# Transposes of the experts' gathered tokens in fp32r in place of fp32

## The chip, the cores and the metric

The kernel runs on one core of a Trainium2 chip. The metric is the device time of one execution in microseconds (us). The core has five engines that work side by side and meet only at semaphores: TensorE (PE, whose weight loads the profile lists apart as PEld), VectorE (DVE), ScalarE (ACT), GpSimd (POOL) and SyncE (SP), which here issues the plain DMAs.

## The reference

One layer is computed on x of shape (4, 2048, 512), that is 8192 tokens of 512 numbers, all in fp32. To x are added an attention-like map of random features and a mixture of experts; both work on the normalised tokens.

```python
xn = _layernorm(x, axis=-1)
x = x + _L0_attn_ref(xn, ...) + _L0_ffn_ref(xn, ...)

# attention: feats(xn) @ feats(input_weights)^T with 512 features
feats = AB / sqrt(512) * exp(einsum('...d,rd->...r', xw, ab[:, None] * gs) - correction)

# experts: 64 of them, 8 a token, chosen among 4 of 8 groups; room for 256 tokens each
g = jnp.einsum('ech,ehi->eci', dispatch, gate_w)
u = jnp.einsum('ech,ehi->eci', dispatch, up_w)
expert_out = jnp.einsum('eci,eih->ech', jax.nn.silu(g) * u, down_w)
output = jnp.zeros((t, h)).at[tidx].add(gathered * weights)
output = output + (silu(tokens @ shared_gate_w) * (tokens @ shared_up_w)) @ shared_down_w
```

`dispatch` holds, for each expert, the rows of the up to 256 tokens that chose it. An expert has 512 inputs and 256 inner units.

## The kernel before

**Precision.** The products are computed in the type fp32r (`FPR`). To keep the accuracy, the kernel splits each operand into an upper part (`upper`, L96, a cast on ACT to fp32r) and a rest (`rest`, L99, a subtraction on DVE). `products` (L102) then adds three products for each pair of operands: upper by upper, upper by rest, rest by upper. That is why the names come in pairs (`gu_h` and `gu_l`, `gT` twice, `d_h` and `d_l`).

**Transposes.** A product sums over the partitions, so tokens that lie one to a partition have to be turned. `nc.tensor.transpose` does it on TensorE: a tile of 128 x 128 is loaded as the weights, and the identity `ident` (L178, fp32) is passed through. The result lands in PSUM. The tiles of the dense blocks are turned in `turn` (L291, product line L299, PSUM tile `ps_x`), the logits at L344 and the experts' tokens in `turn_slots` (L710, product line L717, PSUM tile `ps_t`). All of these are in fp32 before the change.

**Stages.** The tokens pass in 16 blocks of 512 (`NB`). The first stage, up to some 440 us, normalises and turns them (`normalize`, `look_up`), chooses the experts (`look_up`'s later steps), writes the normalised rows with their scores to `xnw` in DRAM, and computes for every other block the shared expert and the attention (`dense`). The second stage is the loop over the 64 experts at L872. The third, from some 1170 us, computes what was left of the odd blocks (`ends`, L836).

**The loop over the experts.** Step i issues the loads of the gate and up weights of expert i + 2 and the down weights of expert i + 1 on SP's queue (L690, L695). It then computes the inner units of expert i (`hidden`, L735: 48 products of 256 columns into `ps_gu`). Next POOL's queue gets the gather of the tokens of expert i + 4 (`gather`, L698, L702), TensorE turns the tokens of expert i + 1 (`turn_slots`), and ACT and DVE split the weights of expert i + 1 (`split_gates`, L589). Late attention work is drawn from a generator (`late_attention`, L533), in 48 pieces of 12 products spread over the 64 steps by L887, so that 16 steps have none. Last come the output product of expert i - 1 (`down`, L753: 12 products of 512 columns into `ps_e`), its scatter with addition to the output on POOL's queue (L767), and the split of the down weights.

**The step around the change.** `turn_slots(e)` takes the gathered rows `xg` (two tiles of 128 tokens, 577 numbers wide) and makes 8 transposes of 128 x 128. Four of them fill one PSUM tile `ps_t` of 512 columns, of which the pool `ps_tr` has two buffers. After each four, ACT casts the tile to the upper part of `gT` (L97) and DVE subtracts for the rest (L100). So an expert has 8 transposes, 2 casts and 2 subtractions, and the stage has 512, 128 and 128.

**What sets the order.** Each engine runs its own queue in order. The order in a queue is planned when the program is built, from the order of the calls and the dependences, and `behind` (L116) adds edges by hand: at L721 the transposes of expert 0 are put behind what TensorE was given before. `in_turn` (L120) keeps POOL's gathers and scatters in sequence. In the profile the planned order shows: most of the time the 8 transposes stand together behind the 48 products of a step, and at times they are spread among other products.

**Constants.** At the start POOL makes `ident`, `tri`, `tri_r` (a cast to fp32r, L183), `ones_r` (L186) and others, one after the other.

Of the kernel before, what the change touches and what calls it, by code (L numbers as in the profile page):

```python
# [9 lines left out]
FP = mybir.dt.float32  # L10
FPR = mybir.dt.float32r
# [7 lines left out]
P = 128  # L19
# [9 lines left out]
CAP = 256  # L29
# [23 lines left out]
def rfs_attention_moe_kernel(  # L53
# [15 lines left out]
    nc = tc.nc  # L69
    xf = x.flatten_outer_dims()  # L70

    const = ctx.enter_context(tc.tile_pool(name="const", bufs=1))
    dram = ctx.enter_context(tc.tile_pool(name="dram", bufs=1, space=DRAM))
    ps_tr = ctx.enter_context(tc.tile_pool(name="ps_tr", bufs=2, space=PSUM))
# [8 lines left out]
    def kib4(shape, name, dt=FPR):  # L83
        return four.tile(shape, dt, tag="four", name=name)
# [11 lines left out]
    def upper(dst, src):  # L96
        return nc.scalar.copy(dst, src)  # L97

    def rest(dst, src, hi, on=nc.vector):  # L99
        return on.tensor_tensor(dst, src, hi.bitcast(FP), ALU.subtract)  # L100
# [15 lines left out]
    def behind(a, b):  # L116

        tc.add_manual_dep(a.ins, b.ins.name, ORDER, reason="what a needs comes late")
# [58 lines left out]

    ident = const.tile([P, P], FP, name="ident")  # L178
    make_identity(nc, ident)
    tri = kib4([P, P], "tri", FP)  # L180
    make_upper_triangular(nc, tri, 1.0, diag=True)
    tri_r = const.tile([P, P], FPR, name="tri_r")
# [426 lines left out]
    for rc in range(RC):  # L609
        ps = ps_mm.tile([P, H], FP, tag="mm", name="ps_f")  # L610
# [98 lines left out]

    def turn_slots(e):  # L710
        xg = xgs.pop(e)
        gp = [kib4([P, KC, CAP], "gT") for _ in range(2)]
        for c2 in range(KC // 2):
            ps = ps_tr.tile([P, 2, CAP], FP, tag="tr", name="ps_t")
            for c in range(2):
                for h in range(NH):
                    turned_s = nc.tensor.transpose(  # L717
                        ps[:, c, ts(h, P)], xg[:, h, ts(c2 * 2 + c, P)], ident
                    )
                    if e == 0:  # L720
                        behind(turned_s, last["pe"])  # L721
            cs = slice(2 * c2, 2 * c2 + 2)
            upper(gp[0][:, cs, :], ps)
            turned_r = rest(gp[1][:, cs, :], ps, gp[0][:, cs, :])

        we = rt.tile([P, NH], FP, tag="we", name="we", bufs=4)
        shares = nc.vector.scalar_tensor_tensor(
            we, xg[:, :, H + e], 1.0, xg[:, :, H + E], ALU.add, ALU.mult
        )
        behind(shares, turned_r)  # L730
        nc.vector.reciprocal(we, we)
        wes[e] = we
        return gp
# [92 lines left out]
    for n in range(NS):  # L826
# [3 lines left out]
        if n == 0:  # L830
            gws[0] = split_gates(gates.pop(0))
    rest_steps -= RC + NS
    gps[0] = turn_slots(0)
    yes = [kib4([P, NH, H], "ye", FP) for _ in range(3)]

# [36 lines left out]
    for i in range(E + 1):  # L872


        if i + 2 < E:
            gates[i + 2] = load_gates(i + 2)
        if i + 1 < E:
            downs[i + 1] = load_down(i + 1)
        if i < E:
            hps[i] = hidden(i, gps.pop(i), gws.pop(i))  # L880
        next(slots, None)
        if i + 4 < E:
            gather(i + 4)
        if i + 1 < E:
            gps[i + 1] = turn_slots(i + 1)
            gws[i + 1] = split_gates(gates.pop(i + 1))
        for _ in range(rest_steps * i // E, rest_steps * (i + 1) // E):  # L887
            next(rest_of, None)
        if i >= E - 2:
            next(last_of)  # L890
        if i == E:

            next(last_of)
        if i > 0:
            down(i - 1, hps.pop(i - 1), dws.pop(i - 1))
        if i < E:
            dws[i] = split_down(downs.pop(i))
# [40 lines left out]
```

## Time and profile before

| what | value |
|---|---|
| median of three executions | 1355.71 us (1353.23 to 1357.19) |
| the profiled execution | 1351.38 us |
| its span, first to last instruction | 1349.6 us |
| mean granted TensorE clock | 0.993 |
| TensorE busy, first stage (0 to 443 us) | 427.36 us |
| TensorE busy, stage of the experts (443 to 1170 us) | 723.46 us |
| TensorE busy, last stage (1170 to 1350 us) | 171.70 us |
| DMA share in these three stages | 0.57, 0.96, 0.73 |

How to read the profile: a group of instructions is one line, with the source line, the engine, the operation, what it writes and reads (out<-in), its form, how often it ran, its busy time in us and the mean of one in ns; behind the second bar stands how long the engine was idle just before, and what ended that. The forms show fp32 and fp32r operands of TensorE alike as f32; a cast shows its fp32r output. The records of TensorE overlap[...]; the time that one costs is therefore the distance between neighbours and not the length of its record. The chain of work that ended last follows the span back from its end, at each step to what released it. A timeline gives the start in us, the time, the engine and the instruction.

### The profile page before, as it was taken

Reading aid. Unit: us, or ns where it says so; the run is one execution under the profiler, and the core shown is the slowest. Engines: PE = TensorE matmul, PEld = TensorE weight load, DVE = VectorE, ACT = ScalarE, POOL = GpSimd, SP = SyncE. Lnnn points to the kernel's source line nnn. Section 1 sums busy time; section 2 is a strip of 40 time slices with the busy share of each in tenths; the row PEclk is TensorE's granted clock in tenths of the full one; section 3 lists DMA queues with packets and bytes.
Section 4 is the critical chain, followed back from the end, with each engine's and each line's share of the span. In section 5 each row is a group of like instructions: output and inputs, shape, how many; then the busy total and the mean of one; then the engine's idle time right before and its main releaser. Section 6 shows DMA issues by size and latency. Waiting matters only on the chain.

```text
span 1349.6 us, 21219 instructions
## 1 busy us (share of the span) xinstructions
PE 1322.5 (98%) x7648; PEld 1153.4 (85%) x7648; DVE 919.5 (68%) x1898; ACT 647.1 (48%) x1025; POOL 580.0 (43%) x683
## 2 busy tenths in 40 slices
PE   7899999999999899999999999999999999999998
PEld 5788888888888799999999999999999999978886
DVE  5887768768765577767677777767776776544455
ACT  5554433443432365556555655655665566531111
POOL 3322022022004566777667676767677655220000
PEclk9899999999999999999999999999999999999999
DMA  7464544564476899999999999999999989756995
GB/s 248 173 231 166 211 184 157 210 222 161 169 268 200 261 243 286 277 270 272 289 268 257 299 287 263 247 283 286 266 263 289 280 235 273 200 143 231 306 316 203
DMA packets 186265, 327.06 MB, mean 242 GB/s; under 512 B 15536, under 2 KB 87216, under 8 KB 186160
## 3 DMA queue, kind: packets, MB, share of 16 engines
q1 hardware_dynamic: 153392, 245.93, 53.0%
q0 software_dynamic: 32768, 79.78, 26.6%
q8 instruction: 60, 0.98, 0.3%
q14 instruction: 45, 0.37, 0.1%
HBM read 220.66 MB, written 104.99 MB: 241 GB/s over the span
## 4 chain that ended last, share of the span: by engine, by line
PE 91%; DMA 3%; DVE 2%; POOL 2%; ACT 1%; issue 1%; SPq 0%; DVEq 0%; POOLq 0%; ACTq 0%
PE ps_gu L107 40%; PE ps_e L107 13%; PE ps_o L107 13%; PE ps_f L107 6%; PE ps_y L107 5%; PE ps_fu L107 5%; PE ps_t L717 4%; PE ps_l L327 2%; PE ps_x L299 2%; DMA at<-upto,line 1%; DMA rw_sb<-in_L_ffn_router_w_dram 1%; POOL at L649 1%; DMA xT_l<-turned 1%; PE ps_lt L344 0%; DVE r L460 0%
## 5 line engine op out<-in xcount | busy, mean ns | idle before, releaser
L107 PE MATMUL ps_gu<-gT,gu_h 128*128 128x256 f32 x2048 | 295.1, 284 | 0.0
L767 POOL DMA_INDIRECT out_dram<-ye,who x128 | 217.4, 1698 | 142.0 <-DMA out_dram<-ye,who 41.1
L107 PEld LDWEIGHTS ps_gu<-gT,gu_h 128*128 128x128 f32 x2048 | 269.3, 192 | 7.0 <-ACT gu_h L97 2.5
L702 POOL DMA_INDIRECT xg<-xnw,who x128 | 143.4, 1121 | 96.1 <-issue 72.1
L649 POOL DMA_INDIRECT at<-upto,line x128 | 148.0, 1156 | 82.5 <-DVE xb L506 43.8
L107 PE MATMUL ps_gu<-gT,gu_l 128*128 128x256 f32 x1024 | 167.1, 285 | 0.0
L100 DVE TENSOR_TENSOR gu_l<-gu,gu_h 128x1024 fp32r<-128x1024 f32 x128 | 155.4, 1216 | 3.8 <-ACT gu_h L97 3.8
L107 PE MATMUL ps_e<-d_h,ehT 128*128 128x512 f32 x512 | 148.8, 392 | 0.0
L107 PEld LDWEIGHTS ps_gu<-gT,gu_l 128*128 128x128 f32 x1024 | 140.9, 192 | 2.8 <-DVE gu_l L100 2.7
L97 ACT CAST gu_h<-gu 128x1024 fp32r<-128x1024 f32 x128 | 131.5, 1056 | 0.0
L97 ACT CAST ehT<-sg 128x512 fp32r<-128x512 f32 x64 | 39.8, 622 | 179.2 <-DVE sg L460 179.2
L228 POOL TENSOR_TENSOR a<-rstd,ve 128x4 f32<-128x4 f32 x48 | 10.9, 227 | 265.4 <-DVE rstd L226 262.8
L107 PEld LDWEIGHTS ps_e<-d_h,ehT 128*128 128x128 f32 x512 | 94.9, 188 | 19.0
L766 ACT ACTIVATE ye<-ps_e,we 128x512 f32<-128x512 f32 x128 | 87.9, 693 | 33.9 <-PE ps_e L107 33.9
L460 DVE SCALAR_TENSOR_TENSOR sg<-sg,ps_gu 128x512 f32<-128x512 f32 x64 | 44.0, 688 | 81.5 <-PE ps_gu L107 81.2
L100 DVE TENSOR_TENSOR d_l<-d,d_h 128x1024 fp32r<-128x1024 f32 x64 | 78.2, 1222 | 11.3 <-ACT d_h L97 11.2
L458 ACT ACTIVATE sg<-ps_gu 128x512 f32<-128x512 f32 x64 | 38.2, 597 | 96.2 <-PE ps_gu L107 95.6
L100 DVE TENSOR_TENSOR gT<-ps_t,gT 128x512 fp32r<-128x512 f32 x128 | 83.3, 682 | 0.4 <-ACT gT L97 0.4
L107 PE MATMUL ps_e<-d_l,ehT 128*128 128x512 f32 x256 | 79.1, 390 | 1.0 <-DVE d_l L100 1.0
L107 PE MATMUL ps_o<-fW_h,fT 128*128 128x512 f32 x288 | 79.7, 391 | 0.3 <-ACT fT L97 0.2
L107 PE MATMUL ps_o<-d_h,hT 128*128 128x512 f32 x256 | 79.8, 399 | 0.0
L717 PE MATMUL ps_t<-ident,xg 128*128 128x128 f32 x512 | 76.1, 275 | 3.5 <-DVE gT L100 3.5
(172 smaller groups left out, 2534.2 us busy)
## 6 DMA issues: line engine op xcount, KB each, us to landing
gu<-in_L_ffn_gate_w_dram SPq DMA_DIRECT2D x64, 512.0 KB
gu<-in_L_ffn_up_w_dram SPq DMA_DIRECT2D x64, 512.0 KB
d<-in_L_ffn_down_w_dram SPq DMA_DIRECT2D x64, 512.0 KB
xnw<-xw SPq DMA_DIRECT2D x32, 577.0 KB
xb<-in_L_attn_x_dram SPq DMA_DIRECT2D x32, 512.0 KB
out_dram<-xb SPq DMA_DIRECT2D x32, 512.0 KB
xT_h<-turned SPq DMA_DIRECT2D x30, 512.0 KB
xT_l<-turned SPq DMA_DIRECT2D x30, 512.0 KB
```

The source lines that it names most:

```text
L97: return nc.scalar.copy(dst, src)
L100: return on.tensor_tensor(dst, src, hi.bitcast(FP), ALU.subtract)
L107: last["pe"] = nc.tensor.matmul(ps, w[c][a], v[c][b], start=(start and part == 0 and c == 0), stop=(stop and part == 2 and c == n - 1),)
L299: last["turn"] = nc.tensor.transpose(ps[:, ts(s, P)], src(s)[:, ts(kc, P)], ident)
L327: logits = nc.tensor.matmul(pl, rwp[:, kc].rearrange("p t e -> p (t e)"), v[kc], start=(n == 0 and kc == 0), stop=(n == 1 and kc == KC - 1),)
L458: nc.scalar.activation(dst, g, AF.Tanh, scale=0.5)
L460: nc.vector.scalar_tensor_tensor(dst, dst, 0.5, u, ALU.mult, ALU.mult)
L649: nc.gpsimd.indirect_dma_start(out=at[:, e % TE, h, :], out_offset=None, in_=upto, in_offset=bass.IndirectOffsetOnAxis(ap=line[:, e, h : h ...
L702: nc.gpsimd.indirect_dma_start(out=xgs[e][:, h, :], out_offset=None, in_=xnw, in_offset=bass.IndirectOffsetOnAxis(ap=who[:, e, h : h + 1], ...
L717: turned_s = nc.tensor.transpose(ps[:, c, ts(h, P)], xg[:, h, ts(c2 * 2 + c, P)], ident)
L766: nc.scalar.activation(ye[:, h, :], po, AF.Copy, scale=wes[e][:, h : h + 1])
L767: now = nc.gpsimd.indirect_dma_start(out=out, out_offset=bass.IndirectOffsetOnAxis(ap=who[:, e, h : h + 1], axis=0), in_=ye[:, h, :], in_o ...
```

## The change

A second identity `ident_r` of type fp32r is made at the start by a cast on POOL. In `turn_slots` the gathered rows are read as fp32r through a bitcast, the transpose uses `ident_r`, and the PSUM tile is allocated as fp32r; ACT and DVE read that tile as fp32 through a bitcast, as before. The other transposes (L299, L344) stay in fp32 with `ident`. No count, no shape and no number of bytes of the 512 transposes is changed.

```diff
@@ -177,6 +177,8 @@
     ident = const.tile([P, P], FP, name="ident")
     make_identity(nc, ident)
+    ident_r = const.tile([P, P], FPR, name="ident_r")
+    nc.gpsimd.tensor_copy(ident_r, ident)
     tri = kib4([P, P], "tri", FP)
@@ -709,13 +711,15 @@
     def turn_slots(e):
         xg = xgs.pop(e)
+        xr = xg.bitcast(FPR)
         gp = [kib4([P, KC, CAP], "gT") for _ in range(2)]
         for c2 in range(KC // 2):
-            ps = ps_tr.tile([P, 2, CAP], FP, tag="tr", name="ps_t")
+            ps_ = ps_tr.tile([P, 2, CAP], FPR, tag="tr", name="ps_t")
+            ps = ps_.bitcast(FP)
             for c in range(2):
                 for h in range(NH):
                     turned_s = nc.tensor.transpose(
-                        ps[:, c, ts(h, P)], xg[:, h, ts(c2 * 2 + c, P)], ident
+                        ps_[:, c, ts(h, P)], xr[:, h, ts(c2 * 2 + c, P)], ident_r
                     )
```

## The prediction

> **What bounds the kernel now.** First the page of the profile, for the engine that fills the span, and its chain of work that ended last:
>
> ```profile
> span 1349.6 us, 21219 instructions
> PE 1322.5 (98%) x7648; PEld 1153.4 (85%) x7648; DVE 919.5 (68%) x1898; ACT 647.1 (48%) x1025; POOL 580.0 (43%) x683
> ...
> PE 91%; DMA 3%; DVE 2%; POOL 2%; ACT 1%; issue 1%; SPq 0%; DVEq 0%; POOLq 0%; ACTq 0%
> PE ps_gu L107 40%; PE ps_e L107 13%; PE ps_o L107 13%; PE ps_f L107 6%; PE ps_y L107 5%; PE ps_fu L107 5%; PE ps_t L717 4%; PE ps_l L327 2%; PE ps_x L299 2%; DMA at<-upto,line 1%; DMA rw_sb<-in_L_ffn_router_w_dram 1%; POOL at L649 1%; DMA xT_l<-turned 1%; PE ps_lt L344 0%; DVE r L460 0%
> ```
>
> TensorE (PE) is the chain, and the transposes concerned, ps_t at L717, are 4% of it. The table of stages, for the stretch in which they all lie:
>
> ```profile
> 443.00:1170.00 727.00, 723.46 (x4845) 662.36 (x4844) 515.04 (x779) 421.28 (x612) 479.23 (x360) 1.00 0.96 268
> ```
>
> The columns after the length are PE, PEld, DVE, ACT and POOL. PE is idle for 3.5 us of 727, at full clock; so time taken from PE here is time off the span, if nobody else becomes late. The second danger is the DMA share, 0.96. The groups of instructions, with shapes apart:
>
> ```profile
> L717 PE MATMUL ps_t<-ident,xg 128*128 128x128 f32 x512 | 76.1, 275 | 3.5 <-DVE gT L100 3.5
> ...
> L717 PEld LDWEIGHTS ps_t<-ident,xg 128*128 128x128 f32 x512 | 59.0, 141 | 8.8 <-DVE gT L100 7.0 <-PE ps_e L107 0.7 <-issue 0.2
> ```
>
> There are 512 transposes. The 275 ns overlap each other, so the price is read from the chain in order of time instead:
>
> ```profile
> 711.61 5.75 PE ps_gu L107 x48
> 717.37 0.87 PE ps_t L717 x8
> 718.24 2.76 PE ps_fu L107 x12
> 721.00 2.72 PE ps_e L107 x12
> ```
>
> Per instruction: ps_gu 120 ns (fp32r, 256 columns), ps_e 227 (fp32r, 512 columns), ps_t 109 (fp32, 128 columns). The two fp32r rows differ by 107 ns for 256 columns, so an fp32r pass costs 13 ns and 0.418 ns a column: by that line 128 columns would be 67 ns, not 109. What holds a transpose at 109, its weight load or its pass? The timeline of weight loads just after an idle TensorE answers that[...]. Three views, narrow windows each: loads of ps_t, the transpose that followed, and loads of an fp32r product.
>
> ```profile
> 458.99 0.14 PEld L717 LDWEIGHTS ps_t<-ident,xg 128*128 128x128 f32 x1 [3.96 <-DVE gT L100]
> ...
> 459.05 0.14 PEld L717 LDWEIGHTS ps_t<-ident,xg 128*128 128x128 f32 x1
> ```
>
> ```profile
> 459.16 0.27 PE L717 MATMUL ps_t<-ident,xg 128*128 128x128 f32 x1
> ```
>
> ```profile
> 247.37 0.19 PEld L327 LDWEIGHTS ps_l<-xT_h,rwp 128*128 128x128 f32 x1 [0.65 <-ACT cu L425]
> ...
> 247.48 0.19 PEld L327 LDWEIGHTS ps_l<-xT_h,rwp 128*128 128x128 f32 x1
> ```
>
> An fp32 transpose loads in about 0.06 us; its pass then runs from 459.05 to 459.16, about 0.11 us. An fp32r product loads 128 columns in 0.11 us. The only fp32r products with 128 columns, ps_u at L417, come each 0.11 us, apart from the first two, which are 0.06 apart:
>
> ```profile
> 61.98 0.22 PE L417 MATMUL ps_u<-tri_r,mask_r 128*128 128x128 f32 x1
> 62.04 0.28 PE L417 MATMUL ps_u<-ones_r,prior_r 128*128 128x128 f32 x1
> 62.15 0.27 PE L417 MATMUL ps_u<-tri_r,mask_r 128*128 128x128 f32 x1
> 62.26 0.27 PE L417 MATMUL ps_u<-ones_r,prior_r 128*128 128x128 f32 x1
> ```
>
> So there are two bounds that happen to agree: the fp32 transpose is held by its **pass** (0.11, load 0.06), the fp32r product by its **load** (0.11, pass 0.06 to 0.07: the first two, and the line above). The change puts the transpose between these rows.
>
> **What the Trainium skill says.** "TensorE: Matmul & The Clock Gate", section "LDWEIGHTS (loading the stationary operand)": columns divided by 1.2, so 107 ns for 128 columns whatever they hold. The trace agrees for fp32r (0.11) and disagrees for the fp32 transpose (0.06). Same page, "Terms": load and matmul have a transpose mode, four times faster for fp32; a load that is quicker in a transpose fits that, though no plain fp32 product stands in this trace. "TensorEngine Tiling (Array Packing)", "Gotcha 2: Feature Incompatibilities", names the transpose mode for FP32/FP32R input, so both types have it; no speed is given. "TensorE: Matmul & The Clock Gate", "Part 4: PE-mode transpose", has about 275 ns for one in a kernel, and no full clock; here the record is as long (275), but they come 109 apart at clock 1.00.
>
> **The change, part by part.**
>
> 1. The 512 transposes. Nothing in number or bytes changes, only the type. No row shows an fp32r transpose. Fast end: the mode sets the load (0.06) and the type sets the pass, pace 67 ns. Slow end with overlap: the type sets both, load-bound like ps_u, 111 ns. Slow end without overlap: load 0.11 and pass 0.06 one after the other, 170 ns. I take the first as the likelier, since the mode is listed for both types and the load seen in that mode is the quick one, but not its full size: 78 ns, a quarter of the way from 67 to 111. That quarter is my choice: a load of some 60 ns under a pace of 67 has hardly any cover, and any start-up of the load beside a pass shows at once.
>
> 2. What of it reaches the path. In the timeline of the stage the 512 stand in 117 runs, broken by other products. The last of a run is followed by an fp32r load of 0.11 us that can only start when that transpose begins, so it gains nothing: 512 - 117 = 395 count, each spaced 109 in the median. 395 x (109 - 78) = 12.2 us less. At the fast end 395 x 42 = 16.6; at the overlapped slow end 512 x 2 = 1 us more.
>
> 3. Who is late next. In 16 of 64 steps no late attention work stands between one expert and the next (48 steps are spread over 64), and PE already waits there for the splits, PEld on gu_l 2.7 us and gu_h 2.5 us in 23 waits. There I expect the gain of a step, 12.2 / 64 = 0.2 us, to be lost: 16 x 0.2 is 3 us if all are, and I take 1 us, since the scheduled order puts other products in the gap. ACT and DVE read the same tiles at the same bytes (gT cast 586 ns, subtraction 682), no change. DMA: the gate load issued at 697.97 feeds a cast at 719.61, over 21 us of lead, and ACT's gu_h cast has 0.0 us idle before it; a stage shorter by 1.7% eats from that lead and not from PE.
>
> 4. ident_r on POOL, once: the neighbouring cast of the same shape (tri_r, L183) takes 0.28 us. PE's first transpose starts at 5.30 with the landing of pj at 5.33, and POOL's last constant (ones_r) is done at 4.62, so 0.7 us cover it; without cover it is 0.3 us. The 512 bytes a partition have no time. The wait of L717 on ident_r is met some 435 us earlier, so nothing queues behind it.
>
> 5. The order of PE's instructions might be planned otherwise with another type. With PE at 99.5% busy in the stage, order alone costs little: up to 2 us either way, kept for the range.
>
> Sum: 12.2 - 1 = 11.2 us less. The profiled execution has 1351.38 us (span 1349.6 and 1.8 around it), so 1340.2; against the median of the runs, 1355.71, that is 1344.5. I forecast **1344 us**.
>
> **The rivals.**
> - *Type sets the load.* Load 0.11, pass 0.06, overlapped: 111 ns, or the compiled instructions stay what they were, 109 ns. Then 0 to 1 us more, and at most 0.3 for POOL: 1356. For it: every fp32r load in the trace takes 0.11, and so does the general price of the skill. Against it: the 0.06 load is the one seen in a transpose.
> - *No overlap* (the slower side). If a transpose in fp32r must finish its own load before, and cannot load beside the pass ahead, it costs 110 + 60 = 170: 512 x 61 = 31 us more, 1387. It decides from a pace of 117 ns (4.1 us / 512 = 8 ns above 109). For it: the two halves change roles and no row shows them together. Against it: ps_u's loads lie beside passes.
> - *The gain is eaten by the splits.* The pace falls to 67 but all of the steps end on ACT and DVE: their queue order after PE's last ps_gu (ehT, gT, gu_h) is unchanged. Then 16.6 us become about 6, at 1350. Against it: 48 of 64 steps have 2.7 us of other PE work there.
>
> **How the numbers follow.** Forecast 0.55 (own range 1336 to 1349), gain eaten 0.05, type sets the load 0.24, no overlap 0.16. A difference within 0.3% (4.1 us) is about what a measurement can't tell from none. Faster: 0.55 + 0.05 = 0.60; same 0.24; slower 0.16. The range 1336 to 1358 leaves out the case without overlap (0.16) and about 0.04 at the fast end.
>
> **What would show it.** Right: in the chain, eight ps_t take 0.5 to 0.7 us instead of 0.87, with loads at 0.06 after an idle PE, and ps_t's share falls from 4% to about 3%. The rival of the load: eight in 0.87 to 0.9, the loads' records near 190 ns instead of 141. No overlap: 1.3 us. Eaten: longer PEld waits on gu_h, gu_l and gT. The prediction is wrong if the pace stays above 101 ns (then less than 4 us is saved), or if DMA waits show on PE in the stage.

## The result and the profile after

The changed kernel takes 1341.91 us in the median of six executions (1338.41 to 1342.59); the kernel before, run beside it, 1353.95 us. The ratio is 0.9903, with a 95% interval of 0.9888 to 0.9917. By the medians it is 12.0 us faster; by the means, which the ratio compares, 13.2. The forecast was 1344 us in a range of 1336 to 1358.

The page of the changed kernel first, with the head of its chain of work:

```profile
span 1339.8 us, 21249 instructions
...
PE 1311.0 (98%) x7648; PEld 1144.8 (85%) x7648; DVE 920.6 (69%) x1898; ACT 645.8 (48%) x1025; POOL 577.3 (43%) x684
...
PE 64%; DMA 1%; DVE 0%; ACT 0%; issue 0%; DVEq 0%
```

TensorE is still the engine that fills the span. The chain is followed back over only 65% of the span here (before: all of it), so its shares are not set against those of before. The stage of the experts, in a window that is ten microseconds shorter, in the table of stages (PE, PEld, DVE, ACT, POOL, clock, DMA share, GB/s):

```profile
443.00:1160.00 717.00, 711.11 (x4839) 652.32 (x4839) 514.40 (x775) 418.22 (x611) 476.38 (x360) 1.00 0.97 271
```

The DMA share goes from 0.96 to 0.97, and no DMA ends a wait of TensorE in the part of the stage after 465 us. The groups of the transposes:

```profile
L721 PE MATMUL ps_t<-ident_r,xg 128*128 128x128 f32 x512 | 58.9, 241 | 5.9 <-DVE gT L100 5.9
L721 PEld LDWEIGHTS ps_t<-ident_r,xg 128*128 128x128 f32 x512 | 52.7, 141 | 11.2 <-DVE gT L100 8.9 <-issue 1.0 <-PE ps_e L107 0.7
```

The record of a weight load is as long as before (141 ns). The one long idle time before ps_t grew from 3.5 to 5.9 us; what it waits for comes in experiment 9. The chain in order of time, one step of the loop:

```profile
710.62 5.75 PE ps_gu L107 x48
716.38 0.63 PE ps_t L721 x8
717.01 2.79 PE ps_fu L107 x12
719.80 2.72 PE ps_e L107 x12
```

Eight transposes end 0.63 us after they began, before 0.87. The 12 products behind them take 2.79 in place of 2.76, so the 20 together save 0.21 us. Summed over 48 of the experts (from the first product of expert 8 to that of expert 56), TensorE's timeline is 551.3 us before and 542.6 after: 0.18 us an expert, or 11.6 for 64.

### The profile page after: what moved, and what is told of

Its sections match the earlier page's. It is cut to its first block, busy times and chain, and to the rows that moved or that the text cites. A ratio compares the mean times of both kernels' runs of the same rounds, so it can differ in the third digit from the quotient of the medians.

```text
span 1339.8 us, 21249 instructions
## 1 busy us (share of the span) xinstructions
PE 1311.0 (98%) x7648; PEld 1144.8 (85%) x7648; DVE 920.6 (69%) x1898; ACT 645.8 (48%) x1025; POOL 577.3 (43%) x684
## 4 chain that ended last, share of the span: by engine, by line
PE 64%; DMA 1%; DVE 0%; ACT 0%; issue 0%; DVEq 0%
PE ps_gu L107 34%; PE ps_e L107 13%; PE ps_y L107 5%; PE ps_fu L107 5%; PE ps_o L107 4%; PE ps_t L721 3%; DMA xT_l<-turned 1%; DMA at<-upto,line 0%; PE ps_f L107 0%; DVE f L454 0%; DVE d_l L100 0%; DVE at L663 0%; ACT f L467 0%; DVE xo L508 0%; ACT fT L97 0%
## 5 line engine op out<-in xcount | busy, mean ns | idle before, releaser
L771 POOL DMA_INDIRECT out_dram<-ye,who x128 | 221.1, 1727 | 143.7 <-DMA out_dram<-ye,who 57.0
L704 POOL DMA_INDIRECT xg<-xnw,who x128 | 136.7, 1068 | 88.7 <-issue 62.6
L462 DVE SCALAR_TENSOR_TENSOR sg<-sg,ps_gu 128x512 f32<-128x512 f32 x64 | 44.0, 688 | 78.7 <-PE ps_gu L107 78.5
L460 ACT ACTIVATE sg<-ps_gu 128x512 f32<-128x512 f32 x64 | 38.4, 600 | 95.8 <-PE ps_gu L107 95.8
L461 DVE SCALAR_TENSOR_TENSOR sg<-sg,ps_gu 128x512 f32<-128x512 f32 x64 | 43.9, 685 | 43.5 <-ACT sg L460 43.4
```

The source lines that it names most:

```text
L460: nc.scalar.activation(dst, g, AF.Tanh, scale=0.5)
L461: nc.vector.scalar_tensor_tensor(dst, dst, 1.0, g, ALU.add, ALU.mult)
L462: nc.vector.scalar_tensor_tensor(dst, dst, 0.5, u, ALU.mult, ALU.mult)
L704: nc.gpsimd.indirect_dma_start(out=xgs[e][:, h, :], out_offset=None, in_=xnw, in_offset=bass.IndirectOffsetOnAxis(ap=who[:, e, h : h + 1], ...
L771: now = nc.gpsimd.indirect_dma_start(out=out, out_offset=bass.IndirectOffsetOnAxis(ap=who[:, e, h : h + 1], axis=0), in_=ye[:, h, :], in_o ...
```

## Experiments

All times are medians; each ratio is one of means, to the kernel before on the same chip, with its 95% interval.

### 1. The new type in the old sequence

When the kernel is built, each engine's order is planned anew, and TensorE's order from the stage of the experts on differs between the two kernels: 1731 of its 7648 products stand at another place. So type and sequence were taken apart. `PLAN` lists the sequence of the kernel before.

```diff
+        made.append(what(*a, **k))        # every product and transpose, as it is called
...
+    planned = [made[k] for first, n in PLAN for k in range(first, first + n)]
+    for b, a in zip(planned[2040:], planned[2041:]):
+        behind(a, b)
```

> The changed kernel, with TensorE's instructions held by added order edges to the very sequence of the kernel before (all other engines free). My theory: the pace inside runs of transposes makes most of the gain (395 transposes x 24 ns, 109 to 85) and TensorE's new sequence the rest (about 2.5 us, by fewer waits for the rests gu_l): 1344.5 us, ratio 0.993 to before. Rival, the gain comes from the new sequence: 1354, ratio 1.000. Rival, the sequence does nothing: 1342, ratio 0.990.

Measured: 1348.9 us, ratio 0.9964 (0.9952 to 0.9976), 4.8 us less than before. That lies between the theory (1344.5) and the rival (1354), so the pace brought less than I had it bring. The runs of transposes did become cheaper: over the 48 experts, with what the first product behind each run takes beyond its usual 120 or 227 ns, they take 43.0 us before, 36.1 after and 36.7 here. But the 48 experts as a whole take 548.6, only 2.7 less than before. The waits of the weight loads from 465 to 1160 us show where it went, first of the kernel before, then of this one (waiting group, what ended the wait; us in total, times, longest):

```profile
PEld ps_t L717 <- DVE gT L100: 3.0, 12, 0.3
PEld ps_gu L107 <- DVE gu_l L100: 2.7, 12, 0.2
PEld ps_gu L107 <- ACT gu_h L97: 2.5, 11, 0.3
```

```profile
PEld ps_t L105 <- DVE gT L100: 6.2, 13, 1.2
PEld ps_gu L105 <- DVE gu_l L100: 3.7, 12, 0.3
PEld ps_gu L105 <- ACT gu_h L97: 2.8, 11, 0.3
```

In the old sequence more than half of what the transposes save turns into waits for ACT's and DVE's splits, in 11 to 13 steps.

### 2. The old type in the new sequence

The same edges in the kernel before, with the changed kernel's sequence as `PLAN`.

> The kernel before, fp32 transposes and all, with TensorE's instructions held to the sequence that the changed kernel has. My theory: only the part that belongs to the sequence, some 2.5 us less, 1351.5, ratio 0.998; ps_t stays at 109 ns apart. Rival, the new sequence is the gain: 1342, ratio 0.990. Rival, the sequence does nothing: 1354, ratio 1.000.

Measured: 1347.3 us, ratio 0.9953 (0.9939 to 0.9966), 6.4 us less, more than the 2.5 that I expected, and far from the 12 of the rival. With fp32 kept, this is the new plan without the new type. All that is left of waits in the same view:

```profile
PEld ps_t L105 <- PE ps_e L105: 0.7, 3, 0.2
PEld ps_t L105 <- issue: 0.3, 1, 0.3
PEld ps_gu L105 <- ACT gu_h L97: 0.2, 1, 0.2
```

The 8.2 us of waits above, for gT, gu_l and gu_h, are gone but for 0.2. The changed kernel itself has 3.1:

```profile
PEld ps_t L721 <- DVE gT L100: 2.6, 12, 0.3
PEld ps_gu L107 <- ACT gu_h L97: 0.5, 2, 0.3
```

The two parts, 4.8 and 6.4, add to 11.2, about the measured 12.0. That they fit so well is in part chance. Over the 48 experts, where all four traces have clock 1.00, the type alone saves 2.7 us (551.3 to 548.6), the new plan alone 3.0 (551.3 to 548.4), and both together 8.7. So the type saves 2.7 us under the old plan and 5.7 under the new one: a third of the gain comes only with both, which fits the waits above: the new plan takes away most of those in which the saving was lost. Outside of these experts the clock plays a part. It was 0.995 in the mean of this run's executions and 0.993 in those of the kernel before; over all executions on record, one with 0.001 more took about 0.7 us less, so by this estimate some 1.5 of the 6.4 us are the clock's.

ACT's and DVE's order was left to the planner in both runs, and it went along with TensorE's. Counted by the tiles that they write, it differs from that of the kernel before at 3 of ACT's 1025 and 2 of DVE's 1898 places in experiment 1, and from that of the changed kernel at 15 and 4 here. What was compared is thus the plan of the three engines; the share of TensorE's sequence in it is not told apart.

### 3 and 8. A plain product in place of the transpose

```diff
-                    turned_s = nc.tensor.transpose(
-                        ps_[:, c, ts(h, P)], xr[:, h, ts(c2 * 2 + c, P)], ident_r
+                    turned_s = nc.tensor.matmul(
+                        ps[:, c, ts(h, P)], xr[:, h, ts(c2 * 2 + c, P)], ident_r,
+                        start=True, stop=True,
                     )
```

> The changed kernel with each transpose done as a plain fp32r product with the identity, not in the transpose mode. It changes part of the computation: the tokens are rounded to fp32r. My theory: the quicker weight load belongs to the transpose mode, so a plain fp32r product loads in 0.11 us and eight take 0.88 us, as in fp32: 1353 to 1356, ratio 1.000. Rival, the type alone makes the pace: eight in 0.63 us, 1342, ratio 0.990.

Measured: 1381.0 us, ratio 1.0211 (1.0195 to 1.0227), 27 us slower, outside both forecasts. Yet the weight loads of a run of eight came as the theory said. The timelines of weight loads below hold one run each; the distance of two loads is the time given less one record, divided by the count less one. First the kernel before, the changed one, and this one:

```profile
717.10 0.90 PEld L717 LDWEIGHTS ps_t<-ident,xg 128*128 128x128 f32 x8
```

```profile
716.11 0.75 PEld L721 LDWEIGHTS ps_t<-ident_r,xg 128*128 128x128 f32 x8
```

```profile
715.90 0.98 PEld L720 LDWEIGHTS ps_t<-ident_r,xg 128*128 128x128 f32 x8
```

(0.90 - 0.14) / 7 = 0.109, (0.75 - 0.14) / 7 = 0.087 and (0.98 - 0.19) / 7 = 0.113 us. So the type alone does not bring the quicker pace; it takes the transpose mode with it. Where most of the 27 us are, the waits of TensorE in the stage show:

```profile
PE ps_gu L107 <- DVE gT L100: 12.5, 14, 0.9
PE ps_gu L107 <- DVE gu_l L100: 5.2, 14, 0.4
PE ps_t L720 <- DVE gT L100: 4.6, 2, 4.4
```

These add to 22 us, where the kernel before has 3.5. This kernel got a plan of its own: in 14 steps without late attention, products of the next expert stand so early that TensorE waits some 0.9 us for gT and soon after 0.4 us for gu_l. To test that, the same kernel was held to the changed kernel's sequence (edges as in experiment 1):

> The third experiment again (a plain fp32r product with the identity, tokens rounded to fp32r), but with TensorE's instructions held to the sequence of the changed kernel. My theory: the 27 us that the third lost were waits of the plan made for it (28 places where TensorE stood over 0.3 us behind the last ps_t), and the product itself costs 112 ns, 2 to 3 more than an fp32 transpose; so this one stands near the second experiment's 1347: 1347 to 1350. Rival, the product in itself costs the 27 us: about 1375.

Measured: 1351.3 us, ratio 0.9977 (0.9966 to 0.9989), 1 us above the forecast. The plan of experiment 3 thus cost 30 us (1381.0 against 1351.3), and the product as such at most 4 us against the fp32 transpose in the same sequence (1351.3 against 1347.3). Even these lie hardly in the products: the 48 experts take 548.7 us here and 548.4 in experiment 2, while the first eight, with the long wait near 460 us (6.4 us here, 3.7 there), take 98.2 and 94.4.

### 4 and 5. Every transpose twice

Doubling is to add 512 transposes inside the runs and no new run. The kernel before, and the changed one:

```diff
+                    for _ in range(2):
                         turned_s = nc.tensor.transpose(...)
```

> The kernel before with each of the 512 transposes done twice in a row, to the same place. The added ones stand inside runs, so they show the pace without the ends of runs. My theory: 109 ns each, 512 x 109 = 56 us more, 1410. If the recorded distance were not the price, say 85 or less in both types: 1397 or less.

> The changed kernel with each of the 512 transposes done twice in a row. My theory: 85 ns each, 512 x 85 = 43.5 us more than the changed kernel's 1342, 1385.5; the distance to the same doubling in fp32 is then 12 + 12.5 = 24.5 us. Rival, the gain does not sit in the pace: both doublings add the same and stay 12 us apart, so 1398.

Measured: 1409.05 us (ratio 1.0400, 1.0371 to 1.0430) and 1385.49 us (1.0232, 1.0204 to 1.0261). The added ones cost (1409.05 - 1352.59) / 512 = 110 ns and (1385.49 - 1341.91) / 512 = 85 ns; both are the recorded distances. The quotients are not as sharp as they look. The 1341.91 comes from the runs of the result, beside which the kernel before took 1353.95 us in place of 1352.59; scaled by that the second would be 88. And each doubled kernel has a plan of its own, with 98 and 96 runs in place of 117 and 120. But the distances of the weight loads in the two traces say the same, (1.77 - 0.14) / 15 = 0.109 us and (0.75 - 0.14) / 7 = 0.087, with medians of 109 and 85 ns:

```profile
702.76 1.77 PEld L718 LDWEIGHTS ps_t<-ident,xg 128*128 128x128 f32 x16
```

```profile
700.46 0.75 PEld L722 LDWEIGHTS ps_t<-ident_r,xg 128*128 128x128 f32 x8
```

So the price of a transpose inside a run is about 109 ns in fp32 and 85 in fp32r.

### 6 and 7. Half a pass, whole weights

Two pieces of 64 rows leave the weights at 128 columns and halve the pass. They tell whether load or pass holds a transpose.

```diff
+                    for q in range(2):
+                        turned_s = nc.tensor.transpose(
+                            ps_[:, c, h * P + q * 64 : h * P + q * 64 + 64],
+                            xr[:64, h, ts(c2 * 2 + c, P)],
+                            ident_r[:64, :64],
+                        )
```

> The kernel before with each transpose split into two of 64 rows (weights still 128 columns, pass of 64 columns), both on the first 64 tokens: the other 64 of each 128 are left out and the first are there twice. My theory, an fp32 transpose is held by its pass: a piece takes about 60 ns (pass 54, load 57), 1024 x 60 = 61 us in place of 56, so 1354 to 1362, unless the change between 128 and 64 rows costs by itself at each run. Rival, it is held by its load: 109 a piece, 56 us more, 1410.

> The changed kernel with the same split into two pieces of 64 rows on the first 64 tokens; the other 64 are left out. My theory, an fp32r transpose is held by its weight load: 85 ns a piece, 1024 x 85 = 87 us in place of 43.5, so 1385. Rival, it is held by its pass[...]: 43 to 60 ns a piece, 1342 to 1360.

Measured: 1395.9 us (1.0308, 1.0273 to 1.0343) and 1417.4 us (1.0467, 1.0430 to 1.0504), in two executions each and both over 30 us above the theory. The pace, though, came out as it said. A run of 16 pieces in fp32, then in fp32r, and the load that followed each:

```profile
700.95 1.08 PEld L718 LDWEIGHTS ps_t<-ident,xg 64*128 64x128 f32 x16
702.10 0.19 PEld L107 LDWEIGHTS ps_e<-d_h,ehT 128*128 128x128 f32 x1
```

```profile
708.62 1.39 PEld L722 LDWEIGHTS ps_t<-ident_r,xg 64*128 64x128 f32 x16
710.05 0.19 PEld L107 LDWEIGHTS ps_e<-d_h,ehT 128*128 128x128 f32 x1
```

The fp32 piece takes (1.08 - 0.14) / 15 = 0.063 us, against 0.109 for the whole: its pass was the bound. The fp32r piece takes (1.39 - 0.14) / 15 = 0.083, no less than the whole: its pass is not the bound. That its weight load is, two more lines show. They hold two loads each behind an idle stretch, of the kernel before and of the changed one, read as the prediction read such pairs:

```profile
687.42 0.20 PEld L717 LDWEIGHTS ps_t<-ident,xg 128*128 128x128 f32 x2 [0.24 <-DVE gT L100]
```

```profile
687.08 0.23 PEld L721 LDWEIGHTS ps_t<-ident_r,xg 128*128 128x128 f32 x2 [0.26 <-DVE gT L100]
```

The second load begins 0.06 us after the first in fp32 and 0.09 in fp32r. Over all such places at full clock the distance is 57 to 62 ns and 83 to 86; in the plain fp32r product of experiments 3 and 8 it is 108.

The rest of the totals is the change of size at each end of a run, which the expectation in fp32 named as a possible cost. In fp32, 1024 x 0.063 in place of 512 x 0.109 is 9 us; 43.3 were measured, so 34 us are left. TensorE's timelines hold them at the ends. From 465 us on, the runs, with what the product at either end takes beyond its usual time, take 55.5 us before and 95.8 here. The 982 pieces in them make 62 us at 63 ns, which leaves 34 us for 101 runs, 0.34 us each. In fp32r it is 118.5 us, 986 pieces at 84 ns make 83, and 36 are left for 119 runs, 0.30 us each. A part can be seen above: the next load begins 0.2 us after the last piece's.

### 9. The routing step behind the splits

The long wait before ps_t near 460 us stands in the kernel before (3.5 us) and in the changed one (5.9). VectorE's timeline of the changed kernel shows why:

```profile
459.84 1.23 DVE L663 TENSOR_TENSOR at<-at,slot 128x1024 f32<-128x1024 f32 x1 [5.98 <-DMA at<-upto,line]
460.98 0.69 DVE L100 TENSOR_TENSOR gT<-ps_t,gT 128x512 fp32r<-128x512 f32 x1
```

A comparison of the routing (`at`) waits for a gather, and the subtraction that frees the PSUM tile stands behind it in the queue. The change (together with an order edge behind the last subtraction):

```diff
-        next(slots, None)
-        if i + 4 < E:
-            gather(i + 4)
         if i + 1 < E:
             gps[i + 1] = turn_slots(i + 1)
             gws[i + 1] = split_gates(gates.pop(i + 1))
+        next(slots, None)
+        if i + 4 < E:
+            gather(i + 4)
```

> The changed kernel with the routing step of a loop turn (next(slots), gather) called behind the turning and splitting for the next expert, so that in VectorE's queue the comparison that waits for the DMA of at no longer stands ahead of the first gT subtraction. My theory: the stall near 455 to 462 us (5.9 us in the changed kernel, with a lower clock just after) goes, the rest of the plan moves a little: 1335 to 1338, ratio 0.988. Rival, the stall only moves to the gather that needs the same tokens, or the new plan costs as much: 1341 to 1344.

Measured: 1334.5 us, ratio 0.9856 (0.9839 to 0.9872): 7.4 us below the changed kernel and the fastest of all. The stage of 440 to 465 us, of the changed kernel and of this one:

```profile
440.00:465.00 25.00, 19.11 (x115) 16.77 (x114) 10.20 (x20) 6.10 (x9) 11.68 (x13) 0.89 0.84 268
```

```profile
440.00:465.00 25.00, 25.00 (x174) 22.51 (x173) 16.93 (x29) 10.76 (x16) 12.68 (x13) 1.00 0.97 312
```

TensorE goes from 19.11 us busy to 25.00 and the clock from 0.89 to 1.00. This kernel has a plan of its own too, but the traces hold the gain at this place: from the first product of expert 0 to that of expert 8 it is 96.2 us in the changed kernel and 87.6 here, and over the 48 experts behind them 542.6 in both. The changed kernel even lost time here, since the kernel before took 94.8 us for those eight. Its wait ends later (461.7 us, before 459.0), and the clock behind it is at 0.50 for 6.8 us, before for 3.4. TensorE's wait is 4.9 us in experiment 1 and 3.7 in experiment 2. Why the gather landed later in some of these kernels was not found.

## Why the prediction was right, point by point

- **What bounds the kernel**: TensorE, and time taken from it comes off the span. Right, as far as the plan lets it: under the old plan 2.7 of 6.3 us did over the 48 experts, under the new one 5.7 of 6.2 (42.3 us for the runs in experiment 2, 36.1 in the changed kernel).
- **The pace (step 1)**: taken as 78 ns, measured 85 (experiment 5). The direction held, the size was off by 7 ns. The ground for it was wrong: I argued that the transpose mode sets a load of 0.06 us and that the pass would then be the bound, with a quarter of the way added by choice. The load is the bound (experiment 7), and at 85 it lies between the fp32 transpose's 57 and the fp32r product's 108. So neither the mode nor the type alone sets it, and the sign that loads would stand 0.06 us apart behind an idle TensorE did not come true. The pass of 67 ns was about right: in the changed kernel the first transposes of a run start 60 and 65 ns apart in the median, before the loads hold them to 84.
- **Held by the pass in fp32**: right, 0.109 whole and 0.063 halved (experiment 6).
- **The last of each run gains nothing (step 2)**: right in the count. Experiment 1 and the changed kernel save 6.3 and 6.9 us on the 380 transposes of the 48 experts, 17 to 18 ns each, where the pace inside a run falls by 24; with one of each of the 86 runs left out that makes 18.6. With the measured pace the term is 395 x 24 = 9.5 us, and not 12.2.
- **Who is late next (step 3)**: I took off 1 us for the splits. In the old sequence more was lost: the runs' saving of 6.3 us shrinks to 2.7 over 48 experts (experiment 1). That is the rival of the eaten gain, in part; its 1350 us is near experiment 1's 1348.9. In the new sequence hardly anything is lost over those experts (5.7 of 6.2).
- **The order (step 5)**: priced at up to 2 us either way. It is the step that failed: the new plan alone brings 6.4 us (experiment 2; 4.6 to 8.3 by its interval), with the new type it brings 7.0 (1348.9 to 1341.9), and the plan of experiment 3 cost 30 against the same kernel in another sequence. That TensorE is busy for 99.5% of the stage says nothing of the gaps that another plan leaves: under that of experiment 3 it was busy for 724.4 of 747 us.
- **ident_r, DMA**: the cast took 0.29 us beside the start, as its row said, and TensorE began at 5.32 us, before at 5.33. No DMA ended a wait of TensorE in the stage after 465 us. But the wait near 460 us, which the prediction showed with its 3.5 us and gave no part, goes back to a gather (experiment 9), and it grew to 5.9.

So the sum (11.2 against 12.0) was better than its parts: the gain of the pace was put too high by 2.7 us, that of the plan too low by more, and the two offset each other. The prediction was right in what bounds the kernel and in the direction. In size it was lucky: the sum of 11.2 us has no gain from a new order, and with the old order kept 4.8 us came (experiment 1).

Of the rivals, the load-bound one was nearest to the truth of the mechanism and wrong in its number, since it took the fp32r product's load for the transpose's. A transpose without overlap (170 ns) did not occur.

## What to carry to other kernels

The price of a transpose here was the larger of two numbers, its load and its pass: 57 and 109 ns in fp32, 85 and about 65 in fp32r. A form that is held by one gains nothing from a quicker other, and halving one of them in an experiment tells which holds. Where the order of an engine is planned at the build, a change of type can also be a change of plan: hold the sequence fixed to tell the two apart, before the whole difference is put down to the instruction. And look in the queue for a wait on a DMA that stands ahead of work that others need: here moving it brought over half as much as the change itself.

## What the runs showed of the hardware

- The weight load of 128 columns of four bytes has three speeds in these kernels: 57 ns for an fp32 transpose, 85 for an fp32r transpose, 108 for an fp32r product, at full clock (experiments 3, 6 and 7).
- The pass of 128 columns takes 109 ns in an fp32 transpose; in fp32r it is under the load's 85, and the first starts of a run stand 60 and 65 ns apart.
- Going from products of 128 rows to a run of 64-row transposes and back cost 0.34 us a run in fp32 and 0.30 in fp32r (experiments 6 and 7). In those traces the next load begins 0.2 us after the last one of the run, where it is 0.11 and 0.09 after whole transposes.
